# Kept combinations of x and W' for rounds P7 and P5, stores on another queue, and a third level for one more pair of steps

## The chip, the cores and the metric

The kernel runs on one core of one Trainium2 chip. The time is the device time of one launch in microseconds (us), median of several runs. A core has five engines that run side by side and wait for each other by semaphores: TensorE (PE: matrix products; PEld is its weight load), VectorE (DVE), ScalarE (ACT), GpSimd (POOL) and SyncE (SP, which issues DMAs). DMAs are issued by the queue of an engine, in that queue's order, and are carried out by 16 transfer engines. Everything here is float32.

## The reference

```python
x = x + ffn0(cond0(x))       # layer 0
x = x + ffn1(cond1(x))       # layer 1
# cond0: out[b] = agg_w[b] (128x128) @ x[b] (128x2048) + agg_b[b],
#        agg_w = softmax(MLP(cond)) @ 8 expert matrices
# ffn0:  y = h @ W.T + bias + sum_e coeffs_e*scales_e * (h @ A_e.T) @ Bf_e.T
# cond1: grouped convolution over the 2048 positions, 9 taps, 4 groups, plus a context bias
# ffn1:  16 heads: t = h[:, perm], t = gelu(t_h @ up_h) @ down_h, back by argsort(perm)
```

x has 32 samples of 128 channels by 2048 positions, that is 4096 rows of 2048. The low-rank part of ffn0 is folded into the weights: W' = W + sum_e w_e Bf_e A_e, so ffn0 is one product of a 4096x2048 and a 2048x2048 matrix. As cond0 mixes channels and ffn0 mixes positions, the kernel forms x W' first and mixes the channels of its result afterwards.

## The kernel before

**The large product.** x W' is computed with the scheme of Winograd's variant of Strassen's algorithm: a 2x2 block product made of seven products P1 to P7 instead of eight, of sums and differences of the blocks. It is used at two levels.

The outer level has seven rounds, in the order `ROUNDS` (line 48): P1, P2, P6, P7, P5, P3, P4. The 4096 rows are cut into `NG` = 8 groups g. A step is one round r and one group g; `steps` runs over all groups of a round, then the next round. For a step the left operand is a block combination of the four tiles x(tp, kh) of its group: `x_load(g, tp, kh)` loads one (128x2048, 1 MB), `x_loads` (line 285) says which a round needs, and `x_combine` (line 296) adds or subtracts them on GpSimd through `pieces` (line 279: four operations of 128x512). Round P6 needs three tiles; its result is also stored to device memory as s2 and read again in P3. The right operand of a round is a combination of blocks of W': `outer_weights` (line 503) loads the four kc parts from `wb_d` and subtracts them on GpSimd. P6's result is stored as t2 for round P4.

The inner level makes seven products again. `x_combine` goes on to form the four combinations of the left operand (tile `s_P`, lines 311 to 314), `inner_weights` (line 245) forms t1, t2, t4 and one more for the right operand, at the end of the round before. `multiply` (line 333) then runs, per step, 7 products of 4 matmuls of 128 by 512 columns, and VectorE adds each finished bank into accumulators (ScalarE copies in the first round). Accumulators of earlier rounds (p1, u1, u2, u3) are loaded by `olds_load` and stored again under the next name by `part_store` (table `ADDED`, line 323).

**The third level.** For a pair of steps (groups g and g+1 of the same round), the products P2 and P4 of both steps can be seen as a 2x2 block product once more. `multiply_third` (line 426) then makes 5 full products in each step and, in the second step, seven quarter products: each of 4 matmuls of 256 columns, with sums from `third_inputs` (tile `sq`, line 410; four operations, on GpSimd or VectorE) and `third_weights` (tiles `P_q`, line 380; the first of the two made on GpSimd, the other on VectorE). The results of the first step are held until the second is done. `in_pair` (line 407) says which pairs do so: rounds in `THIRD`, without those in `SKIP`:

```python
THIRD = ("P2", "P6", "P7", "P5", "P3")
SKIP = (("P2", 3), ("P6", 3), ("P5", 3))
```

(P2, 3) are groups 6 and 7 of round P2.

**The order.** The order of instructions is the program's (a manual schedule): each engine and each queue does its own part in the order in which the program issues it. In step i the loop (from line 1043) issues the left operand of step i+1, in some rounds the x loads of step i+2, then in round P1 two blocks of W' (`w_make_two`), in later rounds the combination of weights that were loaded a step before (`waiting`, line 1083), then the products. Within the products, `between(j)` puts in other work: the small mixed kernels for cond0 on VectorE, loads for the next W' blocks in round P1, and for steps ahead of P6 the x loads of step i+2 (j = 3).

**Memory.** All 1 MB tiles share one pool of 24 slots. A tile gets a slot at build time; its first write waits until the slot's former tile has been read for the last time (also by a DMA that stores it). SyncE's queue, which issues nearly all loads and the accumulators' stores, is in order: a load that waits for its slot keeps back what is behind it. The stores of W' (`w_store`), s2 and t2 are issued by GpSimd's queue, small ag stores by ACT's.

After round P4 come the channel mixing, the convolution and the second layer's 16 heads with indirect gathers and scatters; the change does not touch them.

Of the kernel before, what the change touches and what calls it, by code (L numbers as in the profile page):

```python
# [11 lines left out]
ALU = mybir.AluOpType  # L12
# [36 lines left out]


THIRD = ("P2", "P6", "P7", "P5", "P3")
SKIP = (("P2", 3), ("P6", 3), ("P5", 3))


@with_exitstack
def adaln_ffn_kernel(
# [16 lines left out]
    nc = tc.nc  # L73
# [8 lines left out]
    def slot(name, shape=(P, L)):  # L82
        return big.tile(list(shape), FP, name=name, tag="s")


    def bank():
        return banks.pop(0)

    def done(*ps):
        banks.extend(ps)  # L90
# [4 lines left out]
    def scratch(name, shape=(P, L)):  # L95
        return dram.tile(list(shape), FP, name=name, tag=name)
# [5 lines left out]
        for kh in range(2) for oh in range(2) for kc in range(4)  # L102
    }
    t2_d = {kc: scratch(f"t2_d{kc}") for kc in range(4)}
    w1_d = scratch("w1_d", (1, L))
    red_d = scratch("red_d", (P, L // GC))
    tw_d = scratch("tw_d")
# [1 line left out]
    ag_d = [scratch(f"ag_d{i}") for i in range(B // NCH)]  # L109
    part_d = {  # L110
        (n, g): scratch(f"{n}_d{g}")
        for n in ("s2", "p1", "u1", "u2", "u3", "c00", "c01", "c10", "c11")
        for g in range(NG)
    }

# [150 lines left out]
    def x_load(g, tp, kh):  # L266
        t = slot(f"xt_{g}{tp}{kh}", (P, 2, 2, QW))
        nc.sync.dma_start(t.rearrange("p k s c -> p (k s c)"), xT[g, tp, kh])
        return t

    def part_load(n, g, shape=(P, 2, 2, QW)):
        t = slot(f"{n}_{g}", shape)
        nc.sync.dma_start(t.rearrange("p k s c -> p (k s c)"), part_d[n, g])
        return t

    def part_store(n, g, t, eng=nc.gpsimd):
        eng.dma_start(part_d[n, g], t.rearrange("p k s c -> p (k s c)"))

    def pieces(out, a, b, op):

        for i in range(2):
            for j in range(2):
                nc.gpsimd.tensor_tensor(out[:, i, j], a[:, i, j], b[:, i, j], op)  # L283

    def x_loads(r, g):
        return {
            "P1": lambda: [x_load(g, 0, 0)],
            "P2": lambda: [x_load(g, 0, 1)],
            "P6": lambda: [x_load(g, 1, 0), x_load(g, 1, 1), x_load(g, 0, 0)],
            "P7": lambda: [x_load(g, 0, 0), x_load(g, 1, 0)],  # L290
            "P5": lambda: [x_load(g, 1, 0), x_load(g, 1, 1)],
            "P4": lambda: [x_load(g, 1, 1)],
            "P3": lambda: [x_load(g, 0, 1), part_load("s2", g)],
        }[r]()

    def x_combine(r, g, ts):

        a = ts[0]
        tt = nc.gpsimd.tensor_tensor
        if r == "P6":  # L300

            b, a, c = ts
            pieces(b, b, a, ALU.add)
            pieces(a, b, c, ALU.subtract)
            part_store("s2", g, a)
        if r in ("P7", "P5", "P3"):
            pieces(a, a, ts[1], ALU.add if r == "P5" else ALU.subtract)
        xa[steps.index((r, g))] = a
        s = slot(f"s_{r}{g}", (P, 4, QW))
        a11, a12, a21, a22 = a[:, 0, 0], a[:, 1, 0], a[:, 0, 1], a[:, 1, 1]  # L310
        tt(s[:, 0], a21, a22, ALU.add)  # L311
        tt(s[:, 1], s[:, 0], a11, ALU.subtract)
        tt(s[:, 2], a11, a21, ALU.subtract)
        tt(s[:, 3], a12, s[:, 1], ALU.subtract)
        return {
            "P1": a11, "P2": a12, "P3": s[:, 3], "P4": a22,
            "P5": s[:, 0], "P6": s[:, 1], "P7": s[:, 2],
        }

    xa = {}  # L320
# [12 lines left out]
    def multiply(r, g, lhs, rhs, olds, between):  # L333
        px, py, pz = bank(), bank(), bank()
        accs = olds if olds[0] is not None else [slot(f"m_{r}{g}", (P, 2, 2, QW))]
        fresh = set()

        def add(si, oi, ps):
            for acc in accs:
                to = acc[:, si, oi]  # L340
                if olds[0] is not None or (si, oi) in fresh:
                    nc.vector.tensor_tensor(to, ps, to, ALU.add)  # L342
                else:
                    nc.scalar.copy(to, ps)
            fresh.add((si, oi))

        def product(k, ps, first, last):
            for kc in range(4):
                nc.tensor.matmul(  # L349
                    ps, lhsT=lhs[k][:, bass.ts(kc, P)], rhs=rhs[k][kc],  # L350
                    start=first and kc == 0, stop=last and kc == 3, skip_group_check=True,
                )

        product("P1", px, True, False)
        add(0, 0, px)
        between(0)
        product("P2", pz, True, True)
        add(0, 0, pz)
        done(pz)
        between(1)  # L360
        product("P6", px, False, False)
        add(0, 1, px)
        between(2)
        product("P5", py, True, False)
        add(1, 1, py)
        between(3)
        product("P7", px, False, False)
        add(1, 1, px)
        between(4)
        product("P3", py, False, True)  # L370
        add(0, 1, py)
        done(py)
        between(5)
        product("P4", px, False, True)
        add(1, 0, px)
        done(px)
        for (_, new), acc in zip(ADDED[r], accs):
            part_store(new, g, acc, nc.sync)
# [28 lines left out]
    def in_pair(r, g):  # L407
        return r in THIRD and (r, g // 2) not in SKIP

# [93 lines left out]
    def outer_weights(r, kc):  # L503

        def get(d):
            t = slot(f"wo_{r}{kc}", (P, 2, 2, QW))
            nc.sync.dma_start(t.rearrange("p k o c -> p (k o c)"), d)
            return t

        def w(kh, oh):  # L510
            return wb_d[kh, oh, kc]

        srcs = {
            "P6": [w(1, 1), w(0, 1), w(0, 0)],
            "P7": [w(1, 1), w(0, 1)],
            "P5": [w(0, 1), w(0, 0)],
            "P4": [w(1, 0), t2_d[kc]],
            "P3": [w(1, 1)],
        }[r]
        ts = [get(d) for d in srcs]  # L520

        def combine():
            if len(ts) > 1:
                pieces(ts[0], ts[0], ts[1], ALU.subtract)
            if len(ts) > 2:
                pieces(ts[0], ts[0], ts[2], ALU.add)
                nc.gpsimd.dma_start(t2_d[kc], ts[0].rearrange("p k o c -> p (k o c)"))
            return ts[0]

        return combine  # L530

# [211 lines left out]
    def stage(k, f):  # L743
        for c in range(B // 2):
            n = k - (8 * c - 21)
            if -2 <= n <= 9:
                f(c, n)
# [288 lines left out]
    nxt, waiting, ts = {}, {}, {}  # L1036
# [6 lines left out]
    for i, (r, g) in enumerate(steps):  # L1043
        ri = i // NG
# [54 lines left out]
        def between(j):  # L1099

            b = (ri - 1) * (NG - 2) + g + 1 if ri > 0 else g - (NG - 2)
            if (g in range(1, NG - 1) if ri > 0 else g >= NG - 2) and b < B and j < KEXP // 2:
                mixed_kernel(b, (2 * j, 2 * j + 1))
            if ri == 0 and j == 2:
                for k in blocks[6 + 2 * g : 8 + 2 * g]:
                    wt[k] = w_load(*k)
            if r in THIRD and j < 4 and quarter_ops:
                nc.vector.tensor_tensor(*quarter_ops.pop(0), ALU.subtract)
            if j == 3 and ahead and steps[i + 2][0] == "P6":
                xs[i + 2] = x_loads(*steps[i + 2])  # L1110
            if ri == 0 and j in (1, 3) and unsummed:
                row_sums(*unsummed.pop())
            if ri == 0 and j == 5 and unsummed_first:
                t = unsummed_first.pop(0)
                tt = nc.vector.tensor_tensor
                tt(wsum[:, 0, 0], wsum[:, 0, 0], t[:, 0, 0], ALU.add)
                tt(wsum[:, 0], wsum[:, 0], t[:, 1], ALU.add)
            if last_round:
                if j == 3 and i + 1 < len(steps):
                    lhs[i + 1] = x_combine(*steps[i + 1], xs.pop(i + 1))  # L1120
                    olds_load(i + 1)
                if j in (2, 4):
                    stage(k0 + j // 2, stage_first)
                if j % 2:
                    stage_third(k0 + j // 2)
                else:
                    stage(k0 + j // 2, stage_second)

        if in_pair(r, g):
            multiply_third(  # L1130
                r, g, lhs.pop(i), rhs, olds.pop(i), between, quarters, sq if g % 2 else None
            )
        else:
            multiply(r, g, lhs.pop(i), rhs, olds.pop(i), between)
        xa.pop(i - 1, None)
        if in_pair(r, g) and g % 2 == 0 and (g == 0 or r == "P6"):
            sq = third_inputs(i, nc.vector)
# [13 lines left out]
    for k, (g, h) in enumerate(heads):  # L1151
# [5 lines left out]
        t = ts.pop(k)  # L1157
# [75 lines left out]
```

## Time and profile before

| what | value |
|---|---|
| median of 3 runs | 2601.73 us (2601.64 to 2603.40) |
| the profiled execution | 2603.33 us, of which the span of instructions is 2601.6 |
| granted clock of TensorE, mean | 0.999 |
| round P1 with the making of W' | up to 306.5 us |
| rounds P2, P6, P7, P5 begin at | 306.52, 493.85, 682.88, 868.56 us |
| moved by DMA | 608.28 MB, mean 234 GB/s |
| GpSimd operation of `pieces`, 128x512 | 1.30 us |
| GpSimd operation of `s_P` | 1.29 to 1.38 us |
| VectorE addition of a bank, 128x512 | 0.69 us |
| GpSimd's issue of a store of t_d or s_d | 0.57 us, 0.30 us idle before it |
| the same store, issue to landing | t_d 10.0 us; s_d 6.6 to 10.8, median 9.4 us |

How to read the views: a line of a timeline has the start in us from the span's start, the length in us, engine, source line, operation, the tiles it writes and reads, and how many are merged; in square brackets stands how long the engine was idle before it and what ended that. A line of the waits has who waited, for whom, the total in us, how often, and the longest. "SPq" and "POOLq" are the DMA queues of SyncE and GpSimd. A matmul in float32 appears as two records.

### The profile page before, as it was taken

To read this page: it belongs to the slowest core of one execution; us is meant where nothing else is said; L and a number is where in the kernel's file an instruction comes from. 1 tells how busy PE (TensorE), PEld (TensorE's weight loads), DVE (VectorE), ACT (ScalarE), POOL (GpSimd) and SP (SyncE) were. 2 spreads that over 40 slices of the span, in tenths; PEclk is the share of its full clock that TensorE was granted. 3 is DMA by queue.
4 is the path that set the end of the run, shared out by engine and by line. 5 is a ranking of instruction groups with operands and counts; after the bars stand their busy time and mean duration, and the time that the engine had idled before them with its cause. 6 is when DMAs were issued, how large, how long until landed. Compare 5 with 4: busy or idle time off the path is not lost. (4 is left out here: it accounts for less than half of the span.)

```text
span 2601.6 us, 21348 instructions
## 1 busy us (share of the span) xinstructions
PE 2582.1 (99%) x6876; PEld 1304.0 (50%) x6876; DVE 1476.3 (57%) x2326; ACT 533.6 (21%) x1099; POOL 1322.5 (51%) x1092
## 2 busy tenths in 40 slices
PE   9999999999999999999999999999999999999998
PEld 4444455455455555555454544555545555455543
DVE  5554465356455676544276666667666666666610
ACT  0000000000000000000011244444444444444432
POOL 7321657888986854967323234343444334434232
PEclk9999999999999999999999999999999999999999
DMA  7542458688557487474767797877777877787532
GB/s 311 221 162 99 188 194 331 262 335 324 209 227 290 185 322 299 194 311 162 249 214 259 227 308 260 254 235 226 226 235 236 257 234 222 224 253 236 166 117 89
DMA packets 188160, 608.28 MB, mean 234 GB/s; under 512 B 17680, under 2 KB 92944, under 8 KB 144016
## 3 DMA queue, kind: packets, MB, share of 16 engines
q1 hardware_dynamic: 149936, 473.74, 51.3%
q0 software_dynamic: 32704, 130.04, 14.9%
q10 hardware_dynamic: 5408, 3.13, 0.4%
q8 instruction: 55, 0.90, 0.1%
q14 instruction: 57, 0.47, 0.1%
HBM read 372.45 MB, written 200.84 MB: 220 GB/s over the span
## 5 line engine op out<-in xcount | busy, mean ns | idle before, releaser
L818 PE MATMUL bank<-t,ws 128*128 128x512 f32 x1024 | 460.4, 592 | 0.0
L829 PE MATMUL bank<-gl,ws 128*128 128x512 f32 x1024 | 460.2, 592 | 0.0
L836 POOL DMA_INDIRECT out<-t,orow x128 | 151.0, 1180 | 543.8 <-DVE t L834 482.2
L821 ACT ACTIVATE gl<-bank 128x512 f32<-128x512 f32 x512 | 306.5, 599 | 445.2 <-PE bank L818 435.4
L829 PEld LDWEIGHTS bank<-gl,ws 128*128 128x128 f32 x1024 | 194.6, 190 | 233.0 <-issue 231.0
L818 PEld LDWEIGHTS bank<-t,ws 128*128 128x128 f32 x1024 | 194.5, 190 | 226.9 <-issue 223.0
L567 POOL TENSOR_TENSOR x<-x,fb 128x512 f32<-128x512 f32 x128 | 176.4, 1407 | 224.8 <-DMA x<-in_x 153.8
L834 DVE TENSOR_TENSOR t<-bank,t 128x512 f32<-128x512 f32 x128 | 88.5, 691 | 320.4 <-PE bank L829 320.4
L573 ACT ACTIVATE bank<-w,aggb 128x512 f32<-128x512 f32 x128 | 81.0, 684 | 872.9 <-DMA w<-w_d 855.6
L439 PE MATMUL bank<-P_t,s_P 128*128 128x512 f32 x544 | 241.8, 592 | 0.0
L435 DVE TENSOR_TENSOR u<-bank,u 128x512 f32<-128x512 f32 x168 | 110.7, 688 | 196.2 <-PE bank L439 178.1
L283 POOL TENSOR_TENSOR xt<-xt,xt 128x512 f32<-128x512 f32 x128 | 161.9, 1297 | 106.1 <-DMA xt<-in_xT 88.2
L311 POOL TENSOR_TENSOR s_P<-xt 128x512 f32<-128x512 f32 x56 | 73.3, 1308 | 254.9 <-DMA xt<-in_xT 185.2
L439 PE MATMUL bank<-wo_P,s_P 128*128 128x512 f32 x448 | 199.1, 592 | 0.0
L546 DVE SCALAR_TENSOR_TENSOR ags<-mix,att_bc,ags 128x128 f32<-128x128 f32 x224 | 184.8, 825 | 4.7
L439 PEld LDWEIGHTS bank<-P_t,s_P 128*128 128x128 f32 x544 | 103.4, 190 | 115.6 <-issue 112.4
L802 POOL DMA_INDIRECT t<-hx_d,row x128 | 131.8, 1030 | 53.1 <-issue 25.1
L349 PE MATMUL bank<-P_t,s_P 128*128 128x512 f32 x352 | 154.7, 592 | 0.0
L439 PEld LDWEIGHTS bank<-wo_P,s_P 128*128 128x128 f32 x448 | 85.1, 190 | 95.2 <-issue 92.6
L674 PE MATMUL bank<-va,tw_l 128*128 128x256 f32 x512 | 122.0, 380 | 1.0 <-DVE va L658 1.0
L342 DVE TENSOR_TENSOR u<-bank,u 128x512 f32<-128x512 f32 x84 | 56.4, 685 | 110.0 <-PE bank L349 108.6
L674 PEld LDWEIGHTS bank<-va,tw_l 128*128 128x128 f32 x512 | 96.8, 190 | 43.1 <-issue 32.4
(188 smaller groups left out, 3591.5 us busy)
## 6 DMA issues: line engine op xcount, KB each, us to landing
xt<-in_xT SPq DMA_DIRECT2D x88, 1024.0 KB
u<-u_d SPq DMA_DIRECT2D x40, 1024.0 KB
wo_P<-wb_d SPq DMA_DIRECT2D x36, 1024.0 KB
u<-c_d SPq DMA_DIRECT2D x64, 512.0 KB
x<-in_x SPq DMA_DIRECT2D x32, 1024.0 KB
xg<-x SPq DMA_DIRECT2D x256, 128.0 KB
hx_d<-x1t SPq DMA_DIRECT2D x32, 1024.0 KB
hx_d<-ht SPq DMA_DIRECT2D x32, 1024.0 KB
```

Of the source, the lines that this page charges most:

```text
L283: nc.gpsimd.tensor_tensor(out[:, i, j], a[:, i, j], b[:, i, j], op)
L349: nc.tensor.matmul(ps, lhsT=lhs[k][:, bass.ts(kc, P)], rhs=rhs[k][kc], start=first and kc == 0, stop=last and kc == 3, skip_group_check=True,)
L435: nc.vector.tensor_tensor(acc[:, si, oi], ps, acc[:, si, oi], ALU.add)
L439: nc.tensor.matmul(ps, lhsT=lhs[k][:, bass.ts(kc, P)], rhs=rhs[k][kc], start=first and kc == 0, stop=last and kc == 3, skip_group_check=True,)
L546: nc.vector.scalar_tensor_tensor(ag, mix[:, k], att, ag, ALU.mult, ALU.add)
L567: nc.gpsimd.tensor_tensor(xt[:, f], xt[:, f], late["fb"][:, f], ALU.add)
L674: nc.tensor.matmul(out, lhsT=w[:, 2 * i + r], rhs=rhs, start=first and r == 0, stop=last and r == 1, skip_group_check=True,)
L802: nc.gpsimd.indirect_dma_start(out=t.rearrange("p k t -> p (k t)"), out_offset=None, in_=hx_d[g].rearrange("l k t -> l (k t)"), in_offset= ...
L818: nc.tensor.matmul(pu, lhsT=w[:, m * P : (m + 1) * P], rhs=t[:, 0], start=True, stop=True)
L821: nc.scalar.activation(gl[m], pu, AF.Gelu)
L829: nc.tensor.matmul(pd, lhsT=w[:, (MC + m) * P : (MC + m + 1) * P], rhs=gl[m], start=(m == 0), stop=(m == MC - 1),)
L836: nc.gpsimd.indirect_dma_start(out=out, out_offset=bass.IndirectOffsetOnAxis(ap=orow[:, g, h : h + 1], axis=0), in_=t[:, 1], in_offset=None,)
```

## The change

- `SKIP` loses ("P2", 3), so the last two groups of round P2 use the third level too.
- Round P1, groups g > 1: x(1,0) of the group is loaded beside the products (`other`), subtracted from x(0,0), which is there for the products, and stored as s3. Round P7 then loads s3 for these groups instead of two x tiles and subtracts nothing.
- Round P6: the first of its two combinations, x(1,0) + x(1,1), is stored as s1, and round P5 loads that instead of the two tiles. The final result is written into the tile of x(0,0) instead of that of x(1,1).
- Round P6's weights: the first difference is stored as t3, and P7 loads it instead of two blocks of W'. The sum is written to the third tile instead of the first.
- The stores of s1, s2, t2 and t3 are issued by ACT's queue (s2 and t2 came from GpSimd's before); s3 is stored by GpSimd's.

```diff
-SKIP = (("P2", 3), ("P6", 3), ("P5", 3))
+SKIP = (("P6", 3), ("P5", 3))
...
-            "P7": lambda: [x_load(g, 0, 0), x_load(g, 1, 0)],
-            "P5": lambda: [x_load(g, 1, 0), x_load(g, 1, 1)],
+            "P7": lambda: [part_load("s3", g)] if g > 1 else [x_load(g, 0, 0), x_load(g, 1, 0)],
+            "P5": lambda: [part_load("s1", g)],
...
-            b, a, c = ts
-            pieces(b, b, a, ALU.add)
-            pieces(a, b, c, ALU.subtract)
-            part_store("s2", g, a)
-        if r in ("P7", "P5", "P3"):
-            pieces(a, a, ts[1], ALU.add if r == "P5" else ALU.subtract)
+            b, c, a = ts
+            pieces(b, b, c, ALU.add)
+            part_store("s1", g, b, nc.scalar)
+            pieces(a, b, a, ALU.subtract)
+            part_store("s2", g, a, nc.scalar)
+        elif len(ts) > 1:
+            pieces(a, a, ts[1], ALU.subtract)
...
-            "P7": [w(1, 1), w(0, 1)],
+            "P7": [t3_d[kc]],
...
+            def keep(d, t):
+                nc.scalar.dma_start(d[kc], t.rearrange("p k o c -> p (k o c)"))
+
             if len(ts) > 1:
                 pieces(ts[0], ts[0], ts[1], ALU.subtract)
             if len(ts) > 2:
-                pieces(ts[0], ts[0], ts[2], ALU.add)
-                nc.gpsimd.dma_start(t2_d[kc], ts[0].rearrange("p k o c -> p (k o c)"))
-            return ts[0]
+                keep(t3_d, ts[0])
+                pieces(ts[2], ts[0], ts[2], ALU.add)
+                keep(t2_d, ts[2])
+            return ts[-1 if len(ts) > 2 else 0]
...
+        if ri == 0 and g > 1:
+            other = x_load(g, 1, 0)
         if in_pair(r, g):
...
             multiply(r, g, lhs.pop(i), rhs, olds.pop(i), between)
+        if ri == 0 and g > 1:
+
+            pieces(other, xa[i], other, ALU.subtract)
+            part_store("s3", g, other)
         xa.pop(i - 1, None)
```

More of the change, by code (lines that the diff above doesn't have):

```diff
@@ L104, in adaln_ffn_kernel @@
     t2_d = {kc: scratch(f"t2_d{kc}") for kc in range(4)}
+    t3_d = {kc: scratch(f"t3_d{kc}") for kc in range(4)}
     w1_d = scratch("w1_d", (1, L))
@@ L111, in adaln_ffn_kernel @@
         (n, g): scratch(f"{n}_d{g}")
-        for n in ("s2", "p1", "u1", "u2", "u3", "c00", "c01", "c10", "c11")
+        for n in ("s1", "s2", "s3", "p1", "u1", "u2", "u3", "c00", "c01", "c10", "c11")
         for g in range(NG)
```

## The prediction

> **What bounds the kernel.** I read the page's engine shares first, then TensorE's waits, then the timelines of TensorE, GpSimd and SyncE around the one wait in the rounds that this change touches.
>
> ```profile
> PE 2582.1 (99%) x6876; PEld 1304.0 (50%) x6876; DVE 1476.3 (57%) x2326; ACT 533.6 (21%) x1099; POOL 1322.5 (51%) x1092
> ...
> PE bank L223 <- DVE w L226: 3.2, 3, 2.5
> ...
> PE bank L450 <- POOL P_q L394: 1.4, 1, 1.4
> ...
> PE bank L450 <- POOL P_q L395: 0.5, 1, 0.5
> ```
>
> TensorE is idle for 19.5 of 2601.6 us, mostly before its first products and after its last. Only two waits lie in reach of the change, 1.44 and 0.53 us, both for the GpSimd operands of a third level. So only less TensorE work, or those two waits, can pay; anything else is worth nothing until it makes TensorE wait.
>
> Next, the price of the third level: one stretch of two steps without it (P2, groups 6 and 7), then one with it (P2, groups 0 and 1).
>
> ```profile
> 445.78:493.85 48.07, 48.07 (x114) 21.28 (x113) 14.44 (x23) 0.00 (x0) 36.79 (x32) 1.00 0.70 264
> 306.52:352.94 46.42, 46.42 (x137) 25.84 (x136) 24.16 (x33) 0.59 (x1) 28.34 (x24) 1.00 0.45 177
> ```
>
> Columns: length, then busy time of PE, PEld, DVE, ACT, POOL. TensorE is full in both; the third level is 1.65 us shorter. 28 products of 256 columns (1.73 us per four, 0.433 each) replace 16 of 512 (3.43 per four, 0.858).
>
> Last, the handover from P2 to P6, first on GpSimd, then SyncE, then TensorE.
>
> ```profile
> 442.45 9.93 POOL L283 TENSOR_TENSOR wo_P<-wo_P,wo_P 128x512 f32<-128x512 f32 x8
> 452.69 0.57 POOL L527 DMA_DIRECT2D t_d<-wo_P  x1 [0.30 <-POOL wo_P L283]
> 463.22 9.84 POOL L283 TENSOR_TENSOR xt<-xt,xt 128x512 f32<-128x512 f32 x8 [9.96 <-PE bank L349]
> ...
> 494.63 5.40 POOL L256 TENSOR_TENSOR wo_P<-wo_P 128x512 f32<-128x512 f32 x4
> 500.00 11.18 POOL L283 TENSOR_TENSOR xt<-xt,xt 128x512 f32<-128x512 f32 x8
> 511.48 0.57 POOL L277 DMA_DIRECT2D s_d<-xt  x1 [0.30 <-POOL xt L283]
> ...
> 522.51 0.80 POOL L394 TENSOR_TENSOR P_q<-wo_P,P_q 128x256 f32<-128x256 f32 x1
> ...
> 448.19 2.68 SPq L268 DMA_DIRECT2D xt<-in_xT  x3
> ...
> 521.33 0.59 PE L450 MATMUL bank<-P_q,sq 128*128 128x256 f32 x2
> 523.37 3.29 PE L450 MATMUL bank<-P_q,sq 128*128 128x256 f32 x14 [1.44 <-POOL P_q L394]
> ```
>
> GpSimd works without a gap from 463.22 until P_q is ready at 523.3, and TensorE waits for that. Here GpSimd is the pacer. It started at 463.22 because the third of three x loads, issued by 450.87, had then landed: 12.4 us under four queued megabytes.
>
> **Part 1, a third level for P2, groups 6 and 7.** TensorE: -1.65 us. Around it: VectorE makes 12+7 additions instead of 14, 5 x 0.69 = 3.4 us in a stretch where it is busy 14.4 of 48.1; nothing, and up to 3.4 us if that room were gone. GpSimd makes the four sq operations (1.27 us each, 5.1 in all) between the combination of group 7 and the P6 weights of kc=3. Their cover is the 9.96 us that GpSimd idles before 463.22. The store of c00 for group 6 moves one step later.
> [...]
>
> **Part 2, combinations kept.** Transfers of 1 MB by round: P1 +6 loads (other) and +6 stores (s3); P2 +4 stores (t3); P6 +8 stores (s1), -4 weight loads; P7 -6 x loads; P5 -8. GpSimd operations at 1.30 us: P1 +24, P6 -16 (weights of P7), P7 -24, P5 -32; its issues of DMAs (0.57 plus 0.30 idle before each): -12, +6. GpSimd ends about 60 us less busy, none of it on the path except in two places.
> Round P1 takes its 31 us under TensorE: GpSimd is busy there 8 to 20 us of each 65 between 65 and 260 us, and its operands lead their use by some 20 us (s_P finished at 232.6 for a step that starts at 258.45). If that cover were gone, a step would cost up to 4 x 1.30 + 0.87 = 6.1 us. On SyncE's queue the other load stands ahead of the next W' loads; those are issued at 147.9 to 152.2 and used from 182.7, 30 us later.
> P5's 0.53 us wait goes: the combination before its P_q (L283, 5.5 us at 879.05) is left out. Next late there would be the third-level operands themselves, with 5 us to spare: -0.53.
> P6 steps get stores on ACT's queue. Queued behind them are only the small ag_d stores, whose two buffers VectorE refills two steps (46 us) later; ACT computes nothing in P6. In P2 the first of the new stores stand ahead of ACT's last two Activations for te_d, whose store stands on SyncE (401.29) ahead of loads; they wait for GpSimd until 381.3, 20 us before that. The 16 transfer engines, 0.85 busy at 335 GB/s between 520 and 585 us, get +4 MB in 189 us, 21 GB/s, so about 0.90. Each s_P6 is ready 12 to 18 us ahead of its step (group 3's at 556.6, but its first piece at 547 for a step starting at 559.1), so nothing; a store that holds a slot some 6.6 to 10.8 us (what s_d stores took) is inside that.
>
> **Part 3, the handover, which decides.** In the built program the slots have moved. For P6 group 0, x(1,1) takes the slot of a W' operand that GpSimd frees with its first subtraction of kc=3, and x(0,0) the slot that holds t3 of kc=3 until GpSimd has read it and ACT's store has landed. With sq ahead, that subtraction runs 447.6-452.6 (four at 1.25) and the addition to 457.7.
> - x(1,1) is issued at 452.7. A lone load took 7.1 us (issue 111.14, use 118.28): lands 459.8.
> - the t3 store, issued 452.7, takes between 6.1 us (the wb_d stores) and 10.0 (t_d): x(0,0) is issued 458.8 to 462.7 and lands 466 to 470.
> - GpSimd's first four additions fit before that; the second four take 5, s_P 5.05: ready 476 to 480, against 479.0 before.
> - x loads for group 1 take the slots of P2's t1, t2 and t4, freed by TensorE at about 473, 480 and 484; landed by 491, used at 499.
> - The s_d issue at 511.48 no longer stands on GpSimd: 0.89 us less. P_q is ready at 523.3 - 0.9 + (-3 to +1) = 519.4 to 523.4.
> TensorE, 1.65 us earlier, needs it at 520.1. I take 522.4, nearer the upper end because the loads here share their engines with stores: TensorE resumes 0.9 us earlier than at present and waits 2.2 us. So of the 1.65 only 0.9 arrives; bounds -3.1 (no wait at all) and +0.1.
> [...]
>
> **Sum.** -0.9 (parts 1 and 3) - 0.53 = -1.4 us, bounds -3.6 and -0.4. The profiled run took 2603.33 us (span 2601.6 and 1.7 around it), 1.6 above the median 2601.73; the terms are differences, so I put them on the median: **2600.3**, likeliest own range 2598.1 to 2601.3, plus 0.9 for the scatter of runs (2601.64 to 2603.40).
>
> **Rivals.**
> - No wait is left at P6: 2598.1. For it: GpSimd's 10 us of idle, and fewer loads queued at once. Against: two chained transfers that were parallel before.
> - The gain is eaten: the chain ends 1 to 5 us later than I take, 2601.3 to 2605.3. For it: the load of 12.4 us at this very place.
> - Slower: the same chain at its slowest rows. t3 store 10.8 us, then a 12.4 us load: x(0,0) at 475.9, s_P at 486.0, P_q at 529.4, 6.1 us after today's; less 0.53 that is +5.6, **2607.3**. It decides once x(0,0) lands after 475.6. Against: only two megabytes stand in the queue then.
> - The change does not do what it says: were the pair no shorter, only -0.5 would stay, 2601.2; the 46.42 us of other pairs speak against it.
>
> 0.2%, 5.2 us, is about what a measurement of this kernel can tell from no change. Likeliest 0.50, no wait 0.16 (with 0.03 for more than 5.2 us faster, which no row offers), eaten 0.18, pair without gain 0.03, slower 0.13 (other waits from moved slots in P3 and P4 included). Range 2597.6 to 2605.3: about 0.04 lies below it and 0.15 above. Faster 0.03, same 0.84, slower 0.13.
>
> **What would show it.** P2's last pair 46.4 us long; TensorE's records 6876 + 24 = 6900; the wait of L450 for P_q at P6 about 2.2 us, at P5 none; GpSimd near 1262 us; steps of P1 still 24.0 us. Wrong if TensorE waits in P6 after its first pair, or for s_P or W' in P1, or if P_q at P6 comes after 525.

## The result and the profile after

The changed kernel takes 2608.85 us (median of 20 runs, 2605.30 to 2612.87), the kernel before on the same chips 2602.11 us (20 runs, 2601.36 to 2605.20). The ratio is 1.0024 with a 95% interval of 1.0018 to 1.0031: 6.7 us, a quarter of a per cent, slower. The prediction was 2600.3 us, its range ended at 2605.3.

The profiled execution took 2610.24 us, 6.9 us more than that of before. First the engines' busy shares of the changed kernel, from the page:

```profile
PE 2584.7 (99%) x6900; PEld 1311.6 (50%) x6900; DVE 1469.0 (56%) x2331; ACT 532.7 (20%) x1099; POOL 1268.9 (49%) x1042
```

TensorE has the 24 records more that the third level brings, and GpSimd is 54 us less busy (60 were reckoned). But TensorE is also 2.6 us *more* busy than before, although it has 1.65 us less to do. Its waits in the same kernel (who waits for whom, total us, times, longest):

```profile
PE bank L452 <- POOL P_q L396: 3.8, 2, 2.3
...
PE bank L452 <- DVE u L460: 2.1, 2, 1.9
PE bank L441 <- POOL xt L284: 2.0, 1, 2.0
```

The wait for P_q at P6 has grown from 1.44 to 3.8 us, a wait for a combination of x stands beside it (2.0), and in P5 a wait for VectorE's additions (1.9) stands where before a wait of 0.53 us was, which the profile put down to P_q (what it was for is looked at under "The new wait in P5"). The next view takes two stretches of the changed kernel, P2's last pair of steps and P6's first pair (length; busy time of PE, PEld, DVE, ACT, POOL with their instructions; granted clock; DMA share; GB/s):

```profile
446.62:493.04 46.42, 46.42 (x137) 25.84 (x136) 18.86 (x27) 0.00 (x0) 35.40 (x29) 1.00 0.94 348
493.04:548.43 55.39, 49.64 (x137) 27.34 (x136) 30.12 (x35) 0.00 (x0) 54.63 (x45) 0.94 0.67 268
```

The two pairs make the same products. The first one is exactly as short as predicted, 46.42 us. The second needs 8.97 us more: 5.75 us in which TensorE stands (55.39 - 49.64) and 3.22 us in which it is busy but slow. The reader should look at the clock column: 0.94 in that stretch and 1.00 in the other. The timeline of TensorE shows where:

```profile
512.37 3.70 PE L441 MATMUL bank<-wo_P,xt 128*128 128x512 f32 x8 [1.99 <-POOL xt L284]
...
524.44 0.67 PE L452 MATMUL bank<-P_q,sq 128*128 128x256 f32 x2 [1.49 <-POOL P_q L396]
527.38 5.74 PE L452 MATMUL bank<-P_q,sq 128*128 128x256 f32 x14 [2.27 <-POOL P_q L396]
```

The fourteen records of the last line take 5.74 us; in the kernel before, the same fourteen took 3.29. Between 527 and 532 us the granted clock is 0.50.

What set the lateness is read from the chain of waits of the changed kernel (start, length, what; the pieces in between are GpSimd operations without a gap):

```profile
448.50 4.90 POOL wo_P L284 x4
453.42 15.40 DMA xt<-in_xT
...
478.90 1.27 POOL s_P L313
...
499.92 5.38 POOL wo_P L257 x4
505.31 10.69 POOL xt L284 x8
...
526.60 0.73 POOL P_q L396
527.38 2.93 PE bank L452 x6
```

One load of 1 MB, x(1,1), took 15.4 us. The queues of SyncE and of ACT show what stood before it and beside it:

```profile
430.75 11.18 SPq L509 DMA_DIRECT2D wo_P<-wb_d  x3
442.02 6.44 SPq L278 DMA_DIRECT2D c_d<-p  x2
452.34 0.32 SPq L274 DMA_DIRECT2D p<-p_d  x1
452.75 12.06 SPq L269 DMA_DIRECT2D xt<-in_xT  x3
```

```profile
430.75 5.28 ACTq L526 DMA_DIRECT2D t_d<-wo_P  x2
...
453.42 5.38 ACTq L526 DMA_DIRECT2D t_d<-wo_P  x2
```

- At 430.75 ACT issues the store of t3 for kc=2. The third W' load for kc=3 takes the slot of that very tile, so SyncE stands until 441.6, when the store has landed. Behind it stands the store of c00 for group 4 (442.02; 438.11 before), which lands at 452.28, and only then is its slot free for the load at 452.34 (447.72 before). The x loads go out at 452.75, where before they went out from 448.19.
- At 453.42 both ACT's store of t3 for kc=3 and the load of x(1,1) go out, beside x(1,0), the accumulator's load and the rest of the c00 stores. x(1,1) lands at 468.82.
- x(0,0), whose slot that store holds, goes out at 464.49 and lands at 471.45.

GpSimd starts the combination at 468.98 (463.22 before), has s_P ready at 483.96 (479.0), and from there works without a gap to P_q at 527.3 (523.3).

By the starts of the steps, after minus before in the two profiled executions: 0.85 us before the first step (one execution of each; not pursued), -1.65 in P2's last pair, +7.27 in P6's first pair (55.39 against 48.12), +0.46 in P7, +1.36 in P5's first pair, -1.4 behind that; in all 6.9.

### The profile page after: what moved, and what is told of

It reads as the page before. It is cut to its first block, busy times and chain, and to the rows that moved or that the text cites. A ratio compares the mean times of both kernels' runs of the same rounds, so it can differ in the third digit from the quotient of the medians.

```text
span 2608.5 us, 21370 instructions
## 1 busy us (share of the span) xinstructions
PE 2584.7 (99%) x6900; PEld 1311.6 (50%) x6900; DVE 1469.0 (56%) x2331; ACT 532.7 (20%) x1099; POOL 1268.9 (49%) x1042
## 3 DMA queue, kind: packets, MB, share of 16 engines
q0 software_dynamic: 31840, 123.75, 14.1%
## 4 chain that ended last, share of the span: by engine, by line
PE 87%; POOL 2%; DVE 2%; DMA 1%; issue 1%; POOLq 0%; DVEq 0%
PE bank L441 21%; PE bank L824 17%; PE bank L835 17%; PE bank L351 14%; PE bank L452 8%; PE bank L680 6%; PE bank L588 4%; POOL xt L284 1%; PE bank L224 1%; DMA xt<-in_xT 1%; DVE vb L663 0%; POOL wo_P L257 0%; POOL P_t L254 0%; POOL P_t L253 0%; DVE va L662 0%
## 5 line engine op out<-in xcount | busy, mean ns | idle before, releaser
L441 PEld LDWEIGHTS bank<-P_t,s_P 128*128 128x128 f32 x576 | 109.4, 190 | 122.4 <-issue 119.8
L552 DVE SCALAR_TENSOR_TENSOR ags<-mix,att_bc,ags 128x128 f32<-128x128 f32 x224 | 164.0, 732 | 4.7
L313 POOL TENSOR_TENSOR s_P<-xt 128x512 f32<-128x512 f32 x42 | 55.8, 1328 | 218.8 <-DMA xt<-in_xT 169.3
L284 POOL TENSOR_TENSOR xt<-xt,xt 128x512 f32<-128x512 f32 x96 | 124.2, 1329 | 51.5 <-DMA xt<-in_xT 49.3
L437 DVE TENSOR_TENSOR p<-bank,p 128x512 f32<-128x512 f32 x84 | 56.7, 689 | 125.3 <-PE bank L441 118.7
```

Of the source, the lines that this page charges most:

```text
L437: nc.vector.tensor_tensor(acc[:, si, oi], ps, acc[:, si, oi], ALU.add)
L441: nc.tensor.matmul(ps, lhsT=lhs[k][:, bass.ts(kc, P)], rhs=rhs[k][kc], start=first and kc == 0, stop=last and kc == 3, skip_group_check=True,)
L552: nc.vector.scalar_tensor_tensor(ag, mix[:, k], att, ag, ALU.mult, ALU.add)
```

## Experiments

All kernels were timed beside the kernel before, whose median was 2602.42 us in the first series, 2602.05 in the second and 2602.25 in the third. "s_P" and "P_q" are the ends of these operands for P6 (of P_q, the piece that the fourteen records shown above wait for), "P6" and "P5" are TensorE's waits in the first pair of those rounds, with all waits of the pair added; DVE means a wait for VectorE's additions, and "P_q" is the name that the profile gives. In every kernel whose GpSimd has no added work, P_q is ready 42.8 to 44.3 us after s_P: what is late in s_P is late in P_q.

| kernel | median us | 95% of ratio | s_P | P_q | waits P6 | P5 |
|---|---|---|---|---|---|---|
| before | 2602.05 to 2602.42 | - | 479.0 | 523.3 | 1.44 | 0.53 P_q |
| changed | 2608.85 | 1.0018 to 1.0031 | 484.0 | 527.3 | 5.75 | 1.89 DVE |
| storing only | 2613.36 | 1.0031 to 1.0058 | 480.9 | 523.7 | 4.59 DVE | 1.90 DVE |
| third level only | 2599.13 | 0.9980 to 0.9998 | 475.1 | 518.9 | 0 | 0.53 P_q |
| without t3 | 2599.93 | 0.9982 to 1.0000 | 475.7 | 519.0 | 0 | 1.89 DVE |
| sq on VectorE | 2608.91 | 1.0017 to 1.0036 | 483.0 | 526.5 | 4.04 | 1.87 DVE |
| t3 without kc=3 | 2605.68 | 1.0009 to 1.0029 | 480.6 | 524.1 | 3.51 | 1.89 DVE |
| t3 without kc=2 | 2604.22 | 1.0000 to 1.0018 | 479.6 | 523.1 | 2.12 | 1.88 DVE |
| without t3, sq split | 2597.68 | 0.9974 to 0.9992 | 474.9 | 518.1 | 0 | 0 |
| without t3, P5 g0 combined | 2600.09 | 0.9982 to 1.0000 | 475.8 | 519.0 | 0 | 1.90 DVE |
| without t3, P5 g1 combined | 2598.64 | 0.9976 to 0.9994 | 474.0 | 517.3 | 0 | 0.53 P_q |
| split, P_q 5 operations later | 2600.22 | 0.9983 to 1.0001 | 474.4 | 521.6 | 2.08 | 0 |
| split, P_q 8 operations later | 2604.93 | 1.0001 to 1.0019 | 474.6 | 524.2 | 4.20 | 0 |

### The two halves of the change alone

Theory 1: the stores of t3 hold slots, SyncE's queue stands behind them, the x loads are late. Theory 2: the third level itself, with 5.1 us of sq on GpSimd, makes the handover late. Theory 3: the added traffic slows everything.

Storing only, against the changed kernel:

```diff
-SKIP = (("P6", 3), ("P5", 3))
+SKIP = (("P2", 3), ("P6", 3), ("P5", 3))
```

> All the storing, without the third level of P2's groups 6 and 7 (its four sq operations are gone from GpSimd, TensorE gives up the 1.65 us). Theory 1 (the stores of t3 hold the slots that the next W' load and an x load need, and SyncE's queue stands behind them): SyncE still stands from about 431 to 441 us, the last x load lands after 463, s_P of P6's group 0 is ready after 479 and TensorE waits for it or for P_q as in the kernel before (1.44 us) or up to 3 us more: 2601.5 to 2605. Theory 2 (the third level itself, by its 5.1 us of GpSimd and its slots, makes the handover late): the x loads land by 463, s_P is ready by 479, the wait is 1.5 us or less and only P5's 0.53 us is gained: 2601.6. Theory 3 (more transfers slow everything): steps of P1 or P6 are longer than 24.0 and 24.1 us.

Third level only, against the kernel before:

```diff
-SKIP = (("P2", 3), ("P6", 3), ("P5", 3))
+SKIP = (("P6", 3), ("P5", 3))
```

> The kernel before with the third level of P2's groups 6 and 7 alone; no t3 store, no s1, no s3. Theory 1 (stores of t3 decide): nothing holds SyncE's queue, the last x load lands at 463 to 467, s_P is ready at 479 to 482, TensorE is 1.65 us earlier and waits 1.65 us longer for P_q or up to 3 us more: 2601 to 2605, with P5's 0.5 us still there. Theory 2 (the third level itself): as late as in the changed kernel, s_P after 483 and P_q after 526: 2607 or more. Both: P2's last pair 46.4 us.

The third level alone is 3.3 us *faster* than the kernel before, better than either theory said, and theory 2 falls with it. Its sq operations do delay GpSimd, and so the slots of two of the x loads, but that puts the three loads one after another: 447.58, 451.97, 457.03 us, where before they went out at 448.19, 449.15 and 450.17, with the store of t2 behind them at 452.69. GpSimd can start with the first two at 459.18 instead of 463.22, and the wait of 1.44 us disappears on top of the 1.65 (in the list of TensorE's waits, P5's 0.5 us is the only one of L450 left):

```profile
PE bank L349 <- DVE u L342: 0.9, 1, 0.9
...
PE bank L450 <- POOL P_q L395: 0.5, 1, 0.5
```

Storing alone is the slowest of all. SyncE stood from 430.4 to 440.1 us and s_P came 1.9 us later than before, as theory 1 said, but the 4.59 us wait that follows was in no theory. It is on VectorE, and it is another slot: without sq, the second P_q tile got the slot of group 1's x(1,1), which GpSimd frees at 506.3 with the first half of its combination. (The view below names a DMA; GpSimd's fourth addition runs from 505.05 to 506.32, and VectorE starts 0.03 us later.) VectorE's timeline in that kernel:

```profile
497.32 0.69 DVE L437 TENSOR_TENSOR p<-bank,p 128x512 f32<-128x512 f32 x1 [2.74 <-PE bank L441]
506.35 1.73 DVE L1114 TENSOR_TENSOR P_q<-P_t 128x512 f32<-128x512 f32 x1 [8.33 <-DMA xt<-in_xT]
508.01 0.68 DVE L437 TENSOR_TENSOR p<-bank,p 128x512 f32<-128x512 f32 x1
```

VectorE stands 8.33 us before an operation that is not urgent, and the additions queued behind it keep TensorE's banks. Behind the wait sixteen records took 10.14 us instead of 7.03.

### Taking the suspects out

Without t3, against the changed kernel:

```diff
-            "P7": [t3_d[kc]],
+            "P7": [w(1, 1), w(0, 1)],
...
-                keep(t3_d, ts[0])
```

> The changed kernel without t3: P7's weights are loaded and subtracted anew as in the kernel before, s1 and s3 are stored, the third level stays, the t2 stores stay on ACT. Theory 1: the slots of the W' loads come free as soon as GpSimd has read them, SyncE does not stand from 431 to 441, the x loads land by 466, s_P is ready by 480, P_q by 523.5: 2600 to 2602.5, 6 us under the changed kernel. Theory 2: as the changed kernel, s_P after 483: 2607 to 2609. Theory 3 (contention of the s1 and s3 traffic): between, with no single wait shorter.

The four sq operations on VectorE, against the changed kernel:

```diff
-if in_pair(r, g) and g % 2 == 0 and g > 0 and r != "P6":
+if in_pair(r, g) and g % 2 == 0 and g > 0 and r != "P6" and (r, g) != ("P2", 6):
...
-if in_pair(r, g) and g % 2 == 0 and (g == 0 or r == "P6"):
+if in_pair(r, g) and g % 2 == 0 and (g == 0 or r == "P6" or (r, g) == ("P2", 6)):
```

> The changed kernel with the four sq operations of P2's last pair on VectorE at the end of group 6, instead of on GpSimd; the t3 stores stay. Theory 1: SyncE still stands until about 441, the x loads come as late: the last x load lands at 466 to 471, s_P at 479 to 484, 2605 to 2609. Theory 2: GpSimd starts the x combination 5 us earlier, s_P at 479 or before: 2600 to 2602. VectorE has 30 us of idle in that step; if that cover fails, TensorE shows a wait of L452 on VectorE in P2's group 7.

Without the t3 stores the loss is gone: 8.9 us under the changed kernel, with s1 and s3 stored, and the stores of s2 and t2 on ACT's queue, as in the changed kernel, so theory 3 falls too for that traffic. SyncE's queue no longer stands, and x(1,1), issued at 453.22, is there by 460.41, when GpSimd starts:

```profile
426.62 5.33 SPq L509 DMA_DIRECT2D wo_P<-wb_d  x3
438.75 9.51 SPq L278 DMA_DIRECT2D c_d<-p  x2
448.35 0.38 SPq L274 DMA_DIRECT2D p<-p_d  x1
448.82 9.77 SPq L269 DMA_DIRECT2D xt<-in_xT  x3
```

Moving sq off GpSimd changes nothing (2608.91). GpSimd has the weights done 3.7 us earlier there (454.7 against 458.4) and then waits 11.51 us for x instead of 10.54.

### Which of the two stores

```diff
-            "P7": [t3_d[kc]],
+            "P7": [t3_d[kc]] if kc != 3 else [w(1, 1), w(0, 1)],
...
-                keep(t3_d, ts[0])
+                if kc != 3:
+                    keep(t3_d, ts[0])
```

> The changed kernel, but t3 of kc=3 is not stored (P7 loads and subtracts that quarter's two W' parts anew). The store of kc=2 still holds the slot of the last W' load. If the store of kc=2, by way of SyncE's queue, is the larger half of the delay: SyncE stands from 431 to 441 us as in the changed kernel, the first two x loads go out at 452 to 453, the x combination starts at 464 to 468 and s_P is ready at 479 to 483, TensorE waits 2 to 5 us at P6: 2602 to 2606. If the store of kc=3 that x(0,0) waits for is what matters: s_P by 479, 2600 to 2601.5 as without any t3 store.

The same with 2 in place of 3:

> The changed kernel, but t3 of kc=2 is not stored; that of kc=3 is, and x(0,0) still waits for it. This is the handover as the prediction reckoned it. If the store of kc=2 through SyncE's queue is the larger half: SyncE does not stand from 431 to 441, x(1,0) goes out near 448, x(1,1) near 453 and lands by 463, x(0,0) goes out at 459 to 464 and lands at 466 to 471, s_P is ready at 476 to 481 and P_q at 520 to 525: 2600 to 2604, and 2 us or more under the kernel without the store of kc=3. If the store of kc=3 is what matters: s_P after 482, 2604 to 2608.

By the medians both count. Without kc=3 the kernel is 3.2 us under the changed one, without kc=2 4.6, without any t3 8.9. The runs without kc=3 scatter widely (2601.44 to 2612.03), so there the traces say more than the times: s_P is 3.4 us earlier and the waits at P6 are 2.2 us shorter than in the changed kernel. That kc=2 is the larger half isn't shown: the two kernels are 1.5 us apart, not 2 or more. The kernel without kc=2 is the handover as the prediction reckoned it, with SyncE's queue running: x(1,1), issued at 453.32 in the same moment as the t3 store of kc=3, landed at 464.41, 11.1 us, where without t3 it took at most 7.2. So even there the prediction's 7.1 us was too short. GpSimd starts at 464.57, as x(1,1) has landed; x(0,0), whose slot the store holds, goes out at 463.38 and lands at 469.32, and GpSimd's second four additions follow the first four without a gap. By these rows the kc=3 store costs by running beside x(1,1), and not by the slot that it holds; the two were not separated by a run.

### The new wait in P5

Split sq, against the kernel without t3 (`sq_later` is a list; elsewhere the two operations stay where they were):

```diff
         tt(t[:, 1], t[:, 0], x11, ALU.subtract)
-        tt(t[:, 2], x11, x21, ALU.subtract)
-        tt(t[:, 3], x12, t[:, 1], ALU.subtract)
+        rest = [
+            (t[:, 2], x11, x21, ALU.subtract), (t[:, 3], x12, t[:, 1], ALU.subtract)
+        ]
+        if steps[i] == ("P5", 0):
+            sq_later.extend(rest)
...
         quarter("P5", qy if sq else None, True, False, (1, 1))
+        while g % 2 and sq_later:
+            nc.vector.tensor_tensor(*sq_later.pop(0))
```

> The kernel without t3, and of the four sq operations that VectorE makes between P5's groups 0 and 1 only the first two stay there; the other two are made after the additions for P6's and P5's quarter products, two products before their use. Theory (VectorE's four sq operations, not P_q, set the time of P5's first quarter products): the wait of L452 on VectorE at 895 us (1.89 us) goes, with the half-speed products behind it (1.7 us): 1.9 to 3.6 us under the kernel without t3, 2596.5 to 2598. Rival (something else holds the bank): the wait stays, 2600.

P5's group 0 combined on GpSimd again:

```diff
-            "P5": lambda: [part_load("s1", g)],
+            "P5": lambda: [part_load("s1", g)] if g else [x_load(g, 1, 0), x_load(g, 1, 1)],
...
-            pieces(a, a, ts[1], ALU.subtract)
+            pieces(a, a, ts[1], ALU.add if r == "P5" else ALU.subtract)
```

> The kernel without t3, and P5's group 0 combines its two x loads on GpSimd again as in the kernel before (groups 1 to 7 load s1). Theory (GpSimd's s_P of group 1, which moved beside VectorE's sq operations, slows them from 5.06 to 5.9 us in all, and P_q hid VectorE's additions by 0.1 us before): the wait on VectorE of 1.89 us goes back to 0.53 us on P_q: 1.4 to 3 us under the kernel without t3, 2597 to 2598.5. Rival (VectorE's wait has nothing to do with GpSimd): the 1.89 us stay, 2600.

The same edit with `if g != 1` in place of `if g`:

> The kernel without t3, and P5's group 1 (not group 0) combines its two x loads on GpSimd as in the kernel before: the combination that stood ahead of P_q at 879 us there. GpSimd is then late again and works on P_q, not on s_P of groups 2 and 3, while VectorE makes its four sq operations. Theory (GpSimd's neighbouring operations set VectorE's pace): the sq operations take 5.06 us in all as before and not 5.9, the wait of L452 at P5 is 0.53 us on P_q instead of 1.89 on VectorE: 1.4 us under the kernel without t3, 2598 to 2599. Rival (VectorE is as slow beside any of GpSimd's work): the wait stays near 1.9 us, 2600.

Splitting removed the wait and what came behind it; 2597.68 us is the lowest median of this study, 1.0 us under the next one, which was timed in another series (their intervals overlap). Combining group 0 did nothing, and this run said nothing of the rival: the combination ahead of P_q at 879 us belongs to group 1, so GpSimd did the same work beside VectorE's sq as without the edit. With group 1 combined the wait is 0.53 us again. The timeline of VectorE's four operations in the kernel without t3, then in the one with group 1 combined:

```profile
885.62 0.75 DVE L419 TENSOR_TENSOR sq<-s 128x512 f32<-128x512 f32 x1
886.40 1.64 DVE L420 TENSOR_TENSOR sq<-sq,s 128x512 f32<-128x512 f32 x1
887.96 1.75 DVE L421 TENSOR_TENSOR sq<-s,s 128x512 f32<-128x512 f32 x1
889.63 1.75 DVE L422 TENSOR_TENSOR sq<-s,sq 128x512 f32<-128x512 f32 x1
```

```profile
883.92 1.00 DVE L419 TENSOR_TENSOR sq<-xt 128x512 f32<-128x512 f32 x1
884.95 1.64 DVE L420 TENSOR_TENSOR sq<-sq,s 128x512 f32<-128x512 f32 x1
886.52 1.21 DVE L421 TENSOR_TENSOR sq<-s,xt 128x512 f32<-128x512 f32 x1
887.65 1.21 DVE L422 TENSOR_TENSOR sq<-s,sq 128x512 f32<-128x512 f32 x1
```

The same operations take 1.75 us beside GpSimd's s_P operations (which take 1.71 there, 1.27 alone) and 1.21 beside its half as large P_q operations. The mixing operation behind them is 0.54 us slower as well (1.23 against 0.69). The four operations span 5.76 and 4.94 us. 0.82 + 0.54 = 1.36, which is the difference of the waits (1.89 - 0.53).

That the two differences agree has a reason which the profile's names hide: the 0.53 us were a wait for VectorE's additions too. The kernel before, around the end of that wait:

```profile
895.91 1.27 DVE L458 TENSOR_TENSOR u<-bank,u 128x512 f32<-128x512 f32 x2
896.00 0.73 POOL L395 TENSOR_TENSOR P_q<-wo_P,wo_P 128x256 f32<-128x256 f32 x1
...
896.70 0.30 PEld L450 LDWEIGHTS bank<-P_q,sq 128*128 128x128 f32 x2 [1.32 <-POOL P_q L394]
896.73 0.45 PE L450 MATMUL bank<-P_q,sq 128*128 128x256 f32 x1 [0.53 <-POOL P_q L395]
```

The P_q operation of L395 ends at 896.73, when TensorE's weight load (896.70) has already begun, and the quarter product that starts here (P6) reads what L394 makes, done by 896.05. VectorE's addition of P1's quarter product ended at 896.59 (the first of the two in the first line), and P6's quarter product goes into the same bank (`qx`). TensorE's product resumes 0.14 us after that addition, and it does so too in the kernels with the long wait (in the changed one 905.02 after 904.88, without t3 895.39 after 895.25) and in the one with group 1 combined (892.32 after 892.18).

### What a wait costs beyond its length

In the kernel with split sq the first operation of P6's P_q is repeated, with the same operands, five or eight times:

```diff
+                    for _ in range(5 if name == "P6" and kc == 0 else 0):
+                        tt(t[:, 0, kc], r12, r11, ALU.subtract)
                     tt(t[:, 0, kc], r12, r11, ALU.subtract)
```

> The kernel without t3 and with split sq, in which GpSimd makes the first operation of P6's P_q five times more (same operands, same result), 0.7 to 1.2 us each, so that TensorE waits 2 to 4 us at P6. Theory A (a wait costs its length): the time rises by the length of the wait that the profile shows and the 16 quarter products after it start 0.22 us apart. Theory B (behind a wait of about 2 us or more TensorE runs at half speed for some us): the products after it are 0.43 us apart for 3 to 5 us and the time rises by 1.7 to 2.5 us more than the wait, in some or all of the runs; the runs scatter by more than the 2.1 us of the kernel without the wait.

> As the one with five, but eight operations more: TensorE waits 4 to 7 us. Theory A: the time rises by just that. Theory B: by 1.7 to 2.5 us more than the wait, and in more of the runs than with the shorter wait.

With a wait of 2.08 us the time rises by 2.5 us (2597.68 to 2600.22, timed in different series, whose kernels before were 0.2 us apart); in the profiled run the fourteen records behind it took 3.29 us, full speed (granted clock 1.00). With 4.20 us in two waits it rises by 7.25, 3.05 more than the wait. TensorE's timeline there:

```profile
521.37 0.70 PE L462 MATMUL bank<-P_q,sq 128*128 128x256 f32 x2 [2.01 <-POOL P_q L398]
524.26 4.98 PE L462 MATMUL bank<-P_q,sq 128*128 128x256 f32 x14 [2.19 <-POOL P_q L398]
```

Theory A holds for the short wait within the scatter. In the other kernel the half speed of theory B came: the fourteen records took 4.98 us instead of 3.29, at a granted clock of 0.55 over the 3.80 us from 524.20. That is 1.69 of the 3.05 us; the rest was not located, and the whole is more than theory B's 1.7 to 2.5. As the added time there is two waits with 0.7 us of work between them, no run shows what one long wait of that length costs. The spread of the runs, 2.9 and 3.5 us against 2.1, is larger, but for a single wait only a little.

## Why the prediction was wrong

- **Part 1, the third level: right.** 46.42 us, 6900 records, and alone it is worth 3.3 us: the 1.65 and P6's whole wait of 1.44, which together were part 3's bound of -3.1.
- **Part 2, what moved off GpSimd: about right in its size, 54 us for 60; P1 and the later pairs of P6 kept their lengths.** Theory 3 found nothing.
- **Part 2, P5's wait "goes": wrong.** The step that failed is the reading of the wait as one for P_q, so that it would go because "the combination before its P_q (L283, 5.5 us at 879.05) is left out", with "5 us to spare". The row named P_q, but TensorE was waiting for VectorE's addition of the same bank, as shown above, so leaving out the combination could not take the wait away. It made it longer: GpSimd ran ahead into s_P of the next groups, beside VectorE's sq. The term was -0.53 and measured +1.36.
- **Part 3, the handover: the mechanism was half seen, and its sizes were wrong.** The step that failed first is "A lone load took 7.1 us (issue 111.14, use 118.28): lands 459.8". It put a lone load's price on a load that, by the prediction's own times, goes out together with the t3 store (both 452.7). It took 15.4 us, and 11.1 in the run without the kc=2 store. In the changed kernel five transfers of 1 MB were issued and not landed at 453.42. A better price lay in the trace before, where one row was read wrongly: GpSimd's first four additions need x(1,0) and x(1,1), the first two loads, and so the start at 463.22 tells of the second load, issued at 449.15 (up to 14.1 us), and not of the third (12.4). By the trace's semaphores the second had landed at 463.0 and the third at 465.6. And only the kc=3 store was followed to its slot; the kc=2 store was not, though the W' load behind it on SyncE's queue takes its slot. Without that store alone the kernel is 4.6 us faster. The t3 store took 10.8 us (kc=2) and 11.1 (kc=3), a little over the upper end of the 6.1 to 10.0 reckoned. The last stretch was right: s_P at 484.0 put into the prediction's sum for P_q, 523.3 - 0.9 + (484.0 - 479.0), gives 527.4; it was 527.3. Parts 1 and 3 together, -0.9 in the sum, measured +5.6 (-1.65 and +7.27).
- **The wait's price.** The sum took a wait at its length. In P6, TensorE lost 5.75 us standing and 3.22 us in longer busy time, 2.45 of them in the fourteen records that took 5.74 us for 3.29, at a granted clock of 0.50.
- **The rivals.** "Slower: the same chain at its slowest rows" came close in time (2607.3), but by another path: it needed x(0,0) after 475.6, and x(0,0) landed at 471.45. What was late was the load before it, so the closeness is luck. The sign "P_q at P6 comes after 525" was the right one to watch.

Not tried: a way to keep t3 with its stores from tiles whose slots nothing wants soon. The +0.46 us in P7 and the 0.85 us ahead of the first step were not pursued.

## What to carry to other kernels

A store of a tile that used to die in place kept its slot for 10.8 and 11.1 us more here; follow every such slot to the load that takes it, and that load to all that stands behind it on its queue. Price a transfer by what goes out beside it, not by the quickest row: x(1,1) took 15.4 us in the changed kernel and at most 7.2 in the one without t3. Three loads sent within 2 us, a store close behind, brought their first two operands 4 us later (463.22 against 459.18) than the same three one after another with the store last. Where a wait is to be taken away, hold the name that the profile gives it against the starts and ends around it, look for the second one behind it, and remember that an engine with less work does its other work earlier, beside somebody else: here GpSimd's s_P beside VectorE's sq, of which the last two operations took 1.75 us each instead of 1.21.

## What the runs showed of the hardware

**The clock after a wait.** After some waits TensorE's records came at half speed, those of 256 columns 0.43 us apart instead of 0.22, while the granted clock was 0.50. In the changed kernel this began inside the second of two waits (1.49 and 2.27 us, 0.7 us of work between them, P6) and lasted 6.83 us, from 525.55 to 532.38. With 8 operations more, at the same place after waits of 2.01 and 2.19 us, it lasted about 3.4 us (0.55 over the 3.80 us from 524.20), and as long after one wait of 1.89 us in P5 without t3 (0.51 over 3.50 us). There the clock was still 1.00 up to 896.50, 1.1 us after TensorE had resumed. In two more kernels the times of the records show the slowing: with sq on VectorE, after 1.48 and 2.27 us at P6, fourteen took 4.97 us instead of 3.29, and in storing only, after one wait of 4.59 us, sixteen took 10.14 instead of 7.03. It did not happen after a single wait of 2.08 us at P6 (5 operations more: fourteen records in 3.29 us, clock 1.00), nor after 1.89 and 1.90 us at the same place of P5 in the changed kernel and in the one with group 0 combined (sixteen records in 3.69 us each), nor after 2.46 us near the start of the kernel before (L223, clock 1.00). Each is one execution. The length of the wait alone does not tell the cases apart, 1.89 us being on both sides; what does was not shown. Three stretches of the kernel without t3, columns as above:

```profile
895.30:896.50 1.20, 1.11 (x5) 1.04 (x6) 1.20 (x3) 0.00 (x0) 1.20 (x2) 1.00 0.00 0
896.50:900.00 3.50, 3.50 (x10) 2.76 (x10) 3.46 (x6) 0.00 (x0) 3.42 (x3) 0.51 0.00 0
900.00:904.00 4.00, 4.00 (x12) 2.05 (x11) 1.65 (x3) 0.00 (x0) 1.52 (x2) 1.00 0.00 0
```

**VectorE and GpSimd side by side.** The operations of 128x512 that read two tiles were slower beside each other: VectorE's took 0.68 us alone and 1.75 beside GpSimd's, GpSimd's 1.27 and 1.71, while VectorE's additions from a bank kept their 0.69. Beside each other one pair of operations started every 1.67 us (without t3, 887.96 to 889.63 on VectorE), a little less than the two alone one after the other (0.60 + 1.22 from start to start). What slows them was not shown.
